# Attention block on one core: order of the joins, norm work beside reciprocals, and the place of one copy

## The chip, the core and the metric

The kernel runs on one core of a Trainium2 chip. A core has five engines that work side by side, each through its own queue in order: TensorE (PE in the profile; its weight loads are listed apart as PEld), VectorE (DVE), ScalarE (ACT), GpSimd (POOL) and SyncE (SP), which here only issues DMAs. They wait for each other by semaphores. The metric is the device time of one execution in microseconds; lower is better. A profile of one execution gives every instruction's start and duration, and times below that look like 601.73 are microseconds from the start of that execution's span.

## The reference

Four images of 512 channels and 48 x 48 = 2304 positions go through group normalisation, multi-head self-attention over the positions, a projection and a residual addition:

```python
hn = _group_norm(x, gn_scale, gn_bias)                    # 32 groups
qkv = einsum('oc,bchw->bohw', qkv_w, hn) + qkv_b          # float32
q, k, v = qkv.reshape(b, 3, 8, 64, t).astype(float16)     # 8 heads of 64
w = softmax(einsum('bhct,bhcs->bhts', q * s, k * s))      # s = 64 ** -0.25
a = einsum('bhts,bhcs->bhct', w, v).astype(float32)
out = einsum('oc,bchw->bohw', proj_w, a) + proj_b
return x + out
```

(shortened: `split` of q, k and v along the second axis, bias broadcasts left out.)

## The kernel before

Everything below is the fast path; a general path stands behind a flag and is not taken with these inputs.

**Tiling.** Channels lie on the 128 partitions in NC = 4 chunks. Heads are taken in pairs (two times 64 rows fill the partitions), 4 pairs an image, 16 pairs g in all. Query positions are cut into five blocks j, four of 512 and a last one of 256. A unit of the stream is one pair, one block and BURST = 3 tiles of keys: a block of 512 has six units, the last block three, 27 units a pair and 432 in all. The loop `for n in range(end)` issues one unit of scores each time and works on older units behind it.

**A unit.** `scores` multiplies k and q into PSUM banks ps (L955; three banks in turn) and ScalarE takes the exponential of each into the tile p (L962), three exps of 1024 columns. `values`, two units behind, multiplies v and p into the bank av (L980). The sum of the exponentials, by which the result is divided, is built on VectorE: `add`, one unit behind, adds p into the running sum acc (L1009, 3 x 1024 columns at once). When the block's last unit has been added, the three parts of acc are joined by two more additions of 1024 columns, L1012; those are the joins. Two units later `add_up` sums acc over the partitions with a matmul against ones into the bank sl (L1032), and `rows` copies sl to slx (L1048) and sends the sums by DMA to the tile sums. In the meantime av has been copied to avx (L989). av and sl use one and the same bank in turn, so sl waits for the copy avx, and the next block's av for the copy slx.

**After the block.** Counted from the block's last unit, `invert` comes four units later: it takes the reciprocal of the sums (L1077) and sends it to DRAM; POOL checks the sums' range beside it (L1070, L1071). A unit later `spread` fetches the reciprocals, broadcast over partitions, into the tile ib, and a unit after that `divide` multiplies avx by ib on POOL and writes the pair's result att (L1096). POOL's divisions thus stand six units behind the block's end.

**Work beside the units.** A list `beside` holds the other chains of matmuls in a fixed order: q and k of later pairs (L709, evacuated with bias and scale by VectorE at L719), v (L760, evacuated at L768), and the output projection of the image before (L844, evacuated with bias and residual at L871). Each chain uses the single bank pw, so a chain cannot begin before the one before it has been evacuated. `fill(n)` is called in every unit: it first lets VectorE do some norm tasks of the next image, then issues pieces of chains, paced by a credit so that the list is used up evenly. The norm tasks are statistics (L608, estimated 0.65 us each), their aggregation (L612), the scale of the groups (L622 to L634 with the square root of L631 on POOL), the coefficients (L641 to L653) and the normalisation in place (L660, estimated 0.55 us each). How many of them run is set by `room`, in estimated microseconds; tasks are taken while it is above zero. It is smaller in a unit whose predecessor ended a block (`ended(n - 1)`, where the joins are) and in the one that has the copy slx (`ended(n - BEHIND - 1)`), and larger when the next chain has to wait for the norm itself (`idle`).

**Order in a unit.** VectorE gets, in this order: the addition or, at a block's end, the addition and both joins; then (after `values`) avx; the reciprocal; the norm tasks; the evacuation of the chain that this unit finishes. All of it is issued into VectorE's queue in this order, and the queue is not reordered.

**The projection's input.** Before the chains of a projection, `att32` widens four blocks of att, one for each pair, from 16 to 32 bits (tiles a). Pairs 0 and 1 are copied by ScalarE (L838), pairs 2 and 3 by POOL (L836); `beside_exps` names the pairs of POOL. In the last image some blocks are projected in two parts: the first three pairs (FIRST) early, the last one at the end. A chain reads the pairs in order, two matmuls each (weights split in a high and a low part, whi and wlo).

Of the kernel before, what the change touches and what calls it, by code (L numbers as in the profile page):

```python
# [27 lines left out]
NC = C // P  # L28
# [4 lines left out]
BURST = 3  # L33
BEHIND = 2
# [433 lines left out]
def fast_path(  # L468
# [311 lines left out]
    now = [0]  # L780
# [37 lines left out]
    def left_over(b, j):  # L818

        return b == B - 1 and j >= NQ - 2  # L820

    beside_exps = range(NC // 2, NC)

    def att32(b, j, pairs=range(NC)):
        o, n = QBLOCKS[j]
        for c in pairs:
            if left_over(b, j):
                t = xpool.tile([P, n], F32R, tag=f"x{c}_{j}", name=f"a32_{b}_{j}_{c}")
            else:
                t = work.tile(  # L830
                    [P, QB], F32R, tag=f"a32_{c}", bufs=1, name=f"a32_{b}_{j}_{c}"
                )
            at32[b, j, c] = t[:, :n]
            source = atts[b * NPAIR + c][:, o : o + n]
            if c in beside_exps and not (pairs == LAST and left_over(b, j)):
                nc.gpsimd.tensor_copy(at32[b, j, c], source)  # L836
            else:
                nc.scalar.copy(at32[b, j, c], source)  # L838
# [13 lines left out]
    FIRST, LAST = range(NC - 1), range(NC - 1, NC)  # L852
# [80 lines left out]
    av, acc, pts, avx, sums, rowd, ibs = {}, {}, {}, {}, {}, {}, {}  # L933
# [31 lines left out]
    def values(u):  # L965
# [21 lines left out]
        if last and u is not stream[-1]:  # L987
            avx[g, j] = work.tile([P, QB], F32, tag="avx", name=f"avx_{g}_{j}")
            nc.vector.tensor_copy(avx[g, j][:, :n], av[0][:, :n])  # L989

    def add(u):

        g, j, k, last = u
        pt = pts[u]
        if k == 0:
            acc[g, j] = [pt]
            return
        if j >= NQ - 2 and g == NG - 1 and (last or j == NQ - 1):
            acc[g, j].append(pt)
            return  # L1000
        before = acc[g, j][0]
        if k == 1:
            acc[g, j] = [
                work.tile(
                    [P, BURST, 2, QB], F16, tag="acc", bufs=1, name=f"acc_{g}_{j}"
                )
            ]
        t = acc[g, j][0]
        nc.vector.tensor_tensor(t, before, pt, ALU.add)  # L1009
        if last:  # L1010
            for r in range(1, BURST):
                nc.vector.tensor_tensor(t[:, 0], t[:, 0], t[:, r], ALU.add)  # L1012
            acc[g, j] = [t[:, :1]]

    def add_up(g, j, bank=None, more=False):

# [27 lines left out]
    def rows(g, j, sl):  # L1044

        o, n = QBLOCKS[j]
        sx = work.tile([P, QB], F32, tag="rows", name=f"slx_{g}_{j}")
        nc.vector.tensor_copy(sx[:, :n], sl[:, :n])  # L1048
        sm = small.tile([P, 2, QB // P], F32, tag="sums", name=f"sums_{g}_{j}")
        for h in range(2):  # L1050
            nc.sync.dma_start(sm[:, h, : n // P], sx[h * D : h * D + 1, :n])
        sums[g, j] = sm
        return sx
# [38 lines left out]
        ibs[g, j] = ib  # L1092

    def divide(g, j):
        o, n = QBLOCKS[j]
        nc.gpsimd.tensor_tensor(  # L1096
            atts[g][:, o : o + n],
            avx.pop((g, j))[:, :n],
            ibs.pop((g, j))[:, :n],
            ALU.mult,  # L1100
        )
# [37 lines left out]
    def do_tasks(room):  # L1139
        while tasks and tasks[0][0] <= now[0] and room > 0:  # L1140
            _, us, run = tasks.popleft()
            run()
            room -= us
# [42 lines left out]
    for b in range(B):  # L1186
        g = b * NPAIR
# [113 lines left out]
    def issue():  # L1301
        us, run = beside.pop(0)[:2]
        run()
        credit[0] -= us

    def fill(n):

        idle = beside and beside[0][4] and not beside[0][4]()
        if ended(n - 1):
            room = 1.1 if idle else 0.0
        elif ended(n - BEHIND - 1):
            room = 1.1 if idle else 0.5
        else:
            room = 2.4 if idle else 1.1
        do_tasks(room)
        rate, work = 0.0, 0.0
        for us, _, _, _, _, _, need in beside:  # L1320
            work += us
            left = min(need * per_pair, len(stream) - 4) - n
            rate = max(rate, work / max(left, 1))
        credit[0] = min(credit[0] + rate, 4.0)
        closed = False
        while beside:
            us, _, first, last, when, after, _ = beside[0]
            if after > n or (first and closed) or (when and not when()):
                break
            if us > 0.1 and credit[0] < (0.0 if first and last else us / 2):  # L1330
                break
            issue()
            closed = closed or last

    def wanted(g):

        while any(p[6] <= g for p in beside):
            while loads:
                loads.popleft()[1]()
            while tasks:  # L1340
                tasks.popleft()[2]()
            issue()
            credit[0] = max(credit[0], 0.0)

    ended = lambda n: 0 <= n < len(stream) and stream[n][3]
# [5 lines left out]
    def block_at(n):  # L1351

        return stream[n][:2] if ended(n) and n not in soon else None

    def load_due(n):
        while loads and loads[0][0] <= n:
            loads.popleft()[1]()

    for n in range(end):
        now[0] = n  # L1360
        summed = block_at(n - BEHIND - 1)
        if not summed:
            load_due(n)
        wanted(stream[n][0])
        scores(stream[n])
        if summed:

            rows(*summed, add_up(*summed))
            load_due(n)
        if n > 0:  # L1370
            add(stream[n - 1])
        if summed:

            fill(n)
        if n >= BEHIND:
            values(stream[n - BEHIND])
        if block_at(n - BEHIND - 2):
            check_sums(*block_at(n - BEHIND - 2))
            invert(*block_at(n - BEHIND - 2))
        if block_at(n - BEHIND - 3):  # L1380
            spread(*block_at(n - BEHIND - 3))
        if block_at(n - BEHIND - 4):

            divide(*block_at(n - BEHIND - 4))
        if not summed:
            fill(n)
        if n - BEHIND in soon:
            g, j = stream[n - BEHIND][:2]
            sx = rows(g, j, add_up(g, j))
            if n - BEHIND == soon[1]:  # L1390
                divide_here(g, j, sx, avx[g, j], nc.gpsimd)
        if n - BEHIND - 1 == soon[0]:
            check_sums(g, j)
            invert(g, j)
        if n - BEHIND - 2 == soon[0]:
            spread(g, j)
            divide(g, j)
    g, b, j = NG - 1, B - 1, NQ - 1
    n = QBLOCKS[j][1]
    values(stream[-2])  # L1400
    while loads:
        loads.popleft()[1]()
    check_sums(g, NQ - 2)
    att32(b, NQ - 2, LAST)

    def last_banks(name):
# [5 lines left out]
    sl = held[:, 0, :]  # L1412
    add_up(g, j, sl, more=True)
    add(stream[-1])
    values(stream[-1])
    add_up(g, j, sl)
# [125 lines left out]
```

## Time and profile before

| what | us |
|---|---|
| median of 3 runs | 1608.62 |
| lowest and highest run | 1607.31, 1609.03 |
| the profiled execution | 1608.58 |
| its span, first to last instruction | 1606.8 |
| one exp of 1024 columns (L962), mean | 1.025 |
| one addition of 3072 columns (L1009), mean | 1.794 |
| one join (L1012), mean of 156 | 0.746 |
| one evacuation r (L871), mean of both shapes | 0.693 |
| one POOL division (L1096), mean of both shapes | 1.607 |
| one copy of 512 columns on POOL (L836), mean of 31 | 0.801 |
| the same on ScalarE (L838), mean of 33 | 0.635 |
| one unit of the stream, median distance of two starts of ps | 3.25 |

How to read it: the page lists busy time by engine, the chain of work that ended last (followed back from the last instruction, at each step to what released it), and groups of instructions by line and tile names. Lines in order of time give the start, the duration of what is merged in the line, engine, line, operation, out<-in, shapes and count, and in brackets how long the engine had been idle and who ended that. The page lists idle time of an engine only where something it waited for is seen; matmuls are pipelined, and their ends are modelled. The difference of 1.8 us between the profiled execution and its span lies around the span.

### The profile page before, as it was taken

The numbers are of one execution on the slowest core, as the hardware profiler recorded it, in microseconds if no ns is written. First come the engines' busy times: TensorE is split into PE (matmuls) and PEld (weight loads), VectorE is DVE, ScalarE is ACT, GpSimd is POOL, SyncE is SP. The second block draws the span as 40 slices with busy tenths as digits, with TensorE's granted clock in tenths as the row PEclk, the third lists the DMA queues.
The fourth block names the chain that finished last, engine by engine and source line by source line (L and its number), as shares of the span: only waits on it lengthen the run. The fifth ranks groups of instructions, "written<-read, shape, count | busy, mean of one in ns | idle before, by whom it ended". The sixth has DMA issues, their size and how long they took to land.

```text
span 1606.8 us, 28320 instructions
## 1 busy us (share of the span) xinstructions
PE 1579.1 (98%) x11500; PEld 691.7 (43%) x11500; DVE 1140.3 (71%) x1301; ACT 1267.1 (79%) x1360; POOL 329.5 (21%) x459
## 2 busy tenths in 40 slices
PE   6999999999999999999999999999999999999997
PEld 2533434443333534555333354455533334435554
DVE  6267668866676678887666666898766666667775
ACT  3077777888888888888888888887878888888895
POOL 1011202211121222322111121231212121222232
PEclk9999999999999999999999999999999999999999
DMA  7002021000000024421000001452100000016424
GB/s 220 3 14 65 13 60 28 18 14 11 14 15 14 12 69 119 142 67 28 11 14 18 14 12 41 114 156 84 28 15 15 15 15 11 15 31 188 125 67 128
DMA packets 94896, 82.10 MB, mean 51 GB/s; under 512 B 50852, under 2 KB 60964, under 8 KB 94756
## 3 DMA queue, kind: packets, MB, share of 16 engines
q1 hardware_dynamic: 92724, 78.35, 17.8%
q8 instruction: 92, 1.51, 0.4%
q10 hardware_dynamic: 1904, 1.84, 0.4%
q14 instruction: 48, 0.39, 0.1%
q0 software_dynamic: 128, 0.01, 0.0%
HBM read 60.70 MB, written 19.17 MB: 50 GB/s over the span
## 4 chain that ended last, share of the span: by engine, by line
PE 92%; DVE 3%; DMA 2%; ACT 1%; issue 1%; POOL 1%; SPq 0%; ACTq 0%; DVEq 0%; POOLq 0%
PE pqk L709 29%; PE ps L955 19%; PE av L980 19%; PE pv L760 15%; PE pr L844 7%; PE sl L1032 2%; PE ps L709 1%; ACT p L962 1%; DVE acc L1009 1%; DMA r<-x_dram 1%; DMA wqkv<-qkv_wT_dram 0%; DVE acc L1012 0%; DVE r L871 0%; DMA ib<-row 0%; POOL a L836 0%
## 5 line engine op out<-in xcount | busy, mean ns | idle before, releaser
L962 ACT ACTIVATE p<-ps 128x1024 f16<-128x1024 f32 x1296 | 1233.4, 1025 | 309.2 <-PE ps L955 307.0
L1009 DVE TENSOR_TENSOR acc<-acc,p 128x3072 f16<-128x3072 f16 x270 | 484.3, 1794 | 54.4 <-ACT p L962 51.9
L709 PE MATMUL pqk<-x,wqkv 128*64 128x512 f32 (+1 forms) x2464 | 517.2, 550 | 0.2
L980 PE MATMUL av<-p,v 128*64 128x512 f16 (+1 forms) x2880 | 360.8, 364 | 0.4 <-DVE slx L1048 0.3
L955 PE MATMUL ps<-q,k 64*128 64x512 f16 (+1 forms) x2880 | 356.0, 358 | 1.2 <-ACT p L962 0.8
L760 PE MATMUL pv<-wqkv,x 128*64 128x256 f32 x2304 | 267.5, 379 | 0.0
L709 PEld LDWEIGHTS pqk<-x,wqkv 128*64 128x64 f32 x2464 | 170.1, 137 | 211.1 <-issue 161.0
L1070 POOL TENSOR_SCALAR in<-sums 128x8 f32<-128x8 f32 (+1 forms) x158 | 103.2, 653 | 724.7 <-DMA sums<-slx 718.0
L955 PEld LDWEIGHTS <-k 64*128 64x128 f16 x2880 | 105.9, 94 | 287.9 <-issue 238.9
L980 PEld LDWEIGHTS <-v 128*64 128x64 f16 x2880 | 131.3, 109 | 213.4 <-issue 168.8
L1096 POOL TENSOR_TENSOR att<-avx,ib 128x512 f16<-128x512 f32 (+1 forms) x78 | 125.3, 1607 | 436.9 <-DMA ib<-row 393.9
L760 PEld LDWEIGHTS pv<-wqkv,x 128*64 128x64 f32 x2304 | 161.6, 137 | 85.6 <-DVE v L768 0.6
L1009 DVE TENSOR_TENSOR acc<-p,p 128x3072 f16<-128x3072 f16 x79 | 138.1, 1748 | 0.0
L844 PE MATMUL pr<-a,whi 128*128 128x512 f32 (+1 forms) x311 | 122.0, 400 | 4.0 <-POOL a L836 2.2
L1012 DVE TENSOR_TENSOR acc<-acc 128x1024 f16<-128x1024 f16 x156 | 116.3, 746 | 5.3
L844 PE MATMUL pr<-a,wlo 128*128 128x512 f32 (+1 forms) x311 | 113.6, 373 | 0.0
L719 DVE TENSOR_SCALAR q<-pqk,bqkv 128x512 f16<-128x512 f32 (+1 forms) x79 | 54.7, 693 | 72.6 <-PE pqk L709 72.4
L719 DVE TENSOR_SCALAR k<-pqk,bqkv 128x512 f16<-128x512 f32 (+1 forms) x75 | 52.0, 693 | 73.3 <-PE pqk L709 73.1
L768 DVE TENSOR_TENSOR v<-pv,bv 128x512 f16<-128x512 f32 x72 | 49.5, 688 | 75.4 <-PE pv L760 75.2
L1048 DVE COPY slx<-sl 128x512 f32<-128x512 f32 (+1 forms) x79 | 50.6, 641 | 67.5 <-PE sl L1032 67.5
L989 DVE COPY avx<-av 128x512 f32<-128x512 f32 (+1 forms) x79 | 50.6, 640 | 56.9 <-PE av L980 56.7
L871 DVE SCALAR_TENSOR_TENSOR r<-pr,bproj,r 128x512 f32<-128x512 f32 (+1 forms) x80 | 54.8, 693 | 38.6 <-PE pr L844 36.0
(79 smaller groups left out, 477.0 us busy)
## 6 DMA issues: line engine op xcount, KB each, us to landing
r<-x_dram SPq DMA_DIRECT2D x72, 256.0 KB, 3.7
out_dram<-r SPq DMA_DIRECT2D x69, 256.0 KB, 2.5
ib<-row SPq DMA_DIRECT2D x126, 128.0 KB, 3.1
x<-x_dram SPq DMA_DIRECT2D x62, 256.0 KB, 4.1
x<-x_dram SPq DMA_DIRECT2D x16, 128.0 KB, 4.9
sums<-slx SPq DMA_DIRECT2D x128, 2.0 KB, 2.1
ib<-row SPq DMA_DIRECT2D x30, 64.0 KB, 3.1
wqkv<-qkv_wT_dram SPq DMA_DIRECT2D x2, 768.0 KB, 6.9
```

The lines of the kernel that those rows point to most:

```text
L709: nc.tensor.matmul(pw[0][lo : lo + D, :n], wqkv[:, c, w0 + lo : w0 + lo + D], hn[b, c, j], start=(c == 0), stop=(c == NC - 1),)
L719: nc.vector.tensor_scalar(qk[g][part][:, o : o + n], pw[0][:, :n], bqkv[:, col : col + 1], SCALE, ALU.add, ALU.mult,)
L760: nc.tensor.matmul(pw[0][lo : lo + D, a, :], hn[b, c, i * P // QB][:, at + lo : at + lo + D], wqkv[:, c, 2 * C + half * C // 2 :][:, : C / ...
L844: nc.tensor.matmul(ps[:, :n], w[:, c, bass.ts(m, P)], at32[b, j, c], start=(i == 0), stop=(i == len(steps) - 1),)
L871: nc.vector.scalar_tensor_tensor(xt[:, i], places[i], bias, xt[:, i], ALU.add, ALU.add)
L955: nc.tensor.matmul(ps[:, h, a * n : (a + 1) * n], kt[rows, bass.ts(i, P)], qt[rows, o : o + n], start=True, stop=True,)
L962: nc.scalar.activation(pt[:, r], ps, AF.Exp)
L980: nc.tensor.matmul(av[0][lo : lo + D, :n], vv[b, pr // 2][:, i, pr % 2 * P + lo : pr % 2 * P + lo + D], pt[:, r, h, a * n : (a + 1) * n], ...
L1009: nc.vector.tensor_tensor(t, before, pt, ALU.add)
L1012: nc.vector.tensor_tensor(t[:, 0], t[:, 0], t[:, r], ALU.add)
L1070: nc.gpsimd.tensor_scalar(t, sm, limit, None, op)
L1096: nc.gpsimd.tensor_tensor(atts[g][:, o : o + n], avx.pop((g, j))[:, :n], ibs.pop((g, j))[:, :n], ALU.mult,)
```

## The change

Three edits. `add` issues the first join at once and puts the second into a queue `joins`, which the loop empties behind `fill(n)`, thus behind the evacuation of the chain that this unit finishes. In `fill`, the unit four behind a block's end, the one with the reciprocal, gets the smaller `room` (0.5, or 1.1 when idle, where it had 1.1 and 2.4). `att32` lets ScalarE copy pairs 0, 1 and 2 when a division has been issued in the same unit, and POOL pair 3 alone; in other units the split stays at two and two.

```diff
-    beside_exps = range(NC // 2, NC)
+    divided = [-1]
+
+    def beside_exps():
+
+        return range(NC - 1 if divided[0] == now[0] else NC // 2, NC)
...
-            if c in beside_exps and not (pairs == LAST and left_over(b, j)):
+            if c in beside_exps() and not (pairs == LAST and left_over(b, j)):
...
+    joins = deque()
+
     def add(u):
...
         if last:
-            for r in range(1, BURST):
+            acc[g, j] = [t[:, :1]]
+
+            def join(r):
                 nc.vector.tensor_tensor(t[:, 0], t[:, 0], t[:, r], ALU.add)
-            acc[g, j] = [t[:, :1]]
+
+            for r in range(1, BURST - 1):
+                join(r)
+            joins.append(lambda: join(BURST - 1))
...
     def divide(g, j):
+        divided[0] = now[0]
...
-        elif ended(n - BEHIND - 1):
+        elif ended(n - BEHIND - 1) or ended(n - BEHIND - 2):
             room = 1.1 if idle else 0.5
...
         if not summed:
             fill(n)
+        while joins:
+            joins.popleft()()
```

The order of instructions in the built programs shows what comes of it. TensorE's and SyncE's instructions stand in the same order in both. On VectorE the same 5631 instructions stand in another order: of 78 pairs of joins, 59 now have other work between them. Of the norm work, some statistics and normalisations of images 1 to 3 move to a later unit, and so do the aggregation in images 1 and 3 and the group scale in image 2. Two copies of pair 2 go from POOL to ScalarE: one in image 1, block 2, and one in image 3, block 3.

## The prediction

> **What bounds the kernel now.** I read the page's busy line and chain first, then TensorE's waits, then the order of time at each place where TensorE starts late.
>
> ```profile
> PE 1579.1 (98%) x11500; PEld 691.7 (43%) x11500; DVE 1140.3 (71%) x1301; ACT 1267.1 (79%) x1360; POOL 329.5 (21%) x459
> PE 92%; DVE 3%; DMA 2%; ACT 1%; issue 1%; POOL 1%; SPq 0%; ACTq 0%; DVEq 0%; POOLq 0%
> PE pr L844 <- POOL a L836: 2.2, 3, 1.6
> PE pr L844 <- DVE r L871: 1.0, 2, 0.5
> PE pr L844 <- DVE q L719: 0.6, 1, 0.6
> ```
>
> TensorE is busy for 98% of the span and carries 92% of the chain, at a granted clock of 0.998. So no saving on another engine counts unless TensorE was waiting for it. Its waits in the steady part are few and have names: the copies a (L836) on POOL and the evacuations r and q on DVE. Because matmul ends are modelled, the waits view understates them; I measured them from starts. In an undisturbed unit the first matmul of a chain starts 0.77 us after the first av matmul (0.67 us for a pqk chain after av), and a full projection chain takes 2.06 us from its start to the next ps matmul. What exceeds this is lost. Four places show the kinds of loss.
>
> ```profile
> 1484.08 2.72 POOL L1096 TENSOR_TENSOR att<-avx,ib 128x512 f16<-128x512 f32 x1 [3.69 <-DVE r L871]
> 1485.68 2.39 DVE L1012 TENSOR_TENSOR acc<-acc 128x1024 f16<-128x1024 f16 x2
> 1487.99 0.74 DVE L871 SCALAR_TENSOR_TENSOR r<-pr,bproj,r 128x512 f32<-128x512 f32 x1
> 1488.78 0.50 PE L844 MATMUL pr<-a,whi 128*128 128x512 f32 x1 [0.48 <-DVE r L871]
> ...
> 1039.55 1.26 DVE L608 BATCH_NORM_STATS2 st<-x 128x6 f32<-128x512 f32 x2
> 1040.72 0.47 DVE L719 TENSOR_SCALAR q<-pqk,bqkv 128x256 f16<-128x256 f32 x1
> 1041.24 0.51 PE L844 MATMUL pr<-a,whi 128*128 128x512 f32 x1 [0.55 <-DVE q L719]
> ...
> 1069.50 1.75 DVE L1009 TENSOR_TENSOR acc<-acc,p 128x3072 f16<-128x3072 f16 x1
> 1069.59 3.14 POOL L836 CAST a<-att 128x512 fp32r<-128x512 f16 x2
> 1071.77 0.50 PE L844 MATMUL pr<-a,whi 128*128 128x512 f32 x1 [0.33 <-POOL a L836]
> 1072.79 0.50 PE L844 MATMUL pr<-a,whi 128*128 128x512 f32 x1 [0.28 <-POOL a L836]
> ...
> 1516.23 1.15 ACT L838 CAST a<-att 128x512 fp32r<-128x512 f16 x2
> 1517.26 2.87 ACT L962 ACTIVATE p<-ps 128x1024 f16<-128x1024 f32 x3
> 1517.56 2.34 POOL L1096 TENSOR_TENSOR att<-avx,ib 128x256 f16<-128x256 f32 x1 [7.57 <-DMA ib<-row]
> 1519.85 1.07 POOL L836 CAST a<-att 128x512 fp32r<-128x512 f16 x1
> 1520.97 0.50 PE L844 MATMUL pr<-a,whi 128*128 128x512 f32 x1 [1.58 <-POOL a L836]
> ```
>
> The first shows two joins (L1012), the first of them held up by a POOL division, ahead of an evacuation that TensorE waits for. The second shows two statistics (L608) behind a reciprocal, ahead of an evacuation. The third shows a pair of POOL copies drawn out to 3.14 us beside a DVE addition. The fourth shows a POOL copy behind a division that waited for its DMA.
>
> **What the Trainium skill says.** "SBUF — State Buffer", section "Who interferes with whom": a DVE instruction with two SBUF inputs and a GpSimd instruction that reads SBUF exclude each other, whoever starts first holds the pair for its whole instruction, and PE and ACT never wait there. The trace agrees: a POOL copy of 512 columns takes 0.61 us alone, but the first of the pair above ended 0.47 us after the addition did; a join takes 0.69 us alone and 1.64 to 1.67 us beside a division. The evacuations have one SBUF input at most and stayed at 0.69 to 0.75 us everywhere. "ScalarE: Activation LUTs", section "What ACT_TABLE_LOAD costs": 186 ns plus 0.833 ns a column, back-to-back instructions overlapping by about 93 ns. For 512 columns that is 0.61 us, of which 0.52 us is new time; here a copy takes 0.64 us and its successor starts 0.51 us after it. I use 0.51.
>
> **The change part by part.** TensorE's and SP's instructions keep their order, and TensorE's waits are the same but for two copies that now come from ACT. So nothing is added on the bound; only lateness can change. No DMA is added or moved past another on its queue.
>
> A, the joins. 78 blocks have a second join; in 59 of them other DVE work now stands between the joins, mostly the evacuation. DVE's work is the same, and the evacuation ends up to 0.69 us (join plus gap, 0.72) sooner. It pays where TensorE was late behind it; the excess over 0.77 or 0.67 us: q at 601.73, 0.29 plus 0.05 in its chain; r at 644.55, 0.54; at 677.75, 0.14; at 1097.08, 0.19; at 1466.42, 0.12; at 1488.78, 0.55; at 1542.70, 0.05. Example: at 1488.78 the first join ends at 1487.34, the evacuation can follow at 1487.38 and end at 1488.12, and 0.05 us of handover (as between 1488.73 and 1488.78) gives 1488.17, before TensorE's own 1488.23. Each of the others fits in the same way; the sum is 1.93 us. The first join stays ahead and may still meet the lock, so 1.5 to 1.95. The second join now delays avx, L989, behind it: no cost, because avx cannot begin before the last av matmul is done. At 601 us the old second join ended at 601.02; the new one runs from 600.94 to 601.63, avx still starts at 601.72. If that cover went, sl (first matmul at 604.36) still leaves 1.9 us. Two late evacuations stay, since nothing before them changes: v at 278.91 behind the coefficients (0.32) and r at 655.80, which starts with DVE idle (0.13).
>
> B, the norm work. In the unit of the reciprocal one statistic instead of two is issued; the rest moves one unit on. At 1041.24 the loss over 0.77 is 0.62. With one statistic (0.68) after 1039.55, q ends at about 1040.60, TensorE starts at 1040.65 against 1040.62: gain 0.60, at least 0.3 if the sums' DMA behind the reciprocal comes later. The pushed-on work costs nothing where DVE idles before the next evacuation (r at 1043.42 waited 0.56 us for TensorE). The tightest place is near 1069 us, where the aggregation (four instructions, 0.64 us) now shares a unit with the group scale: r there ends at about 1070.13 to 1070.22 instead of 1069.58, and TensorE needs it at 1070.19. I take nothing; 0.05 is the bound there, and up to 1.5 us for such places that I have not found.
>
> C, the third copy on ACT. It applies twice only, in the units of 1068 and 1516 us. At 1516: the chain starts at 1518.19 and a six-matmul chain takes 1.60 us (1523.16 to 1524.76), so ps would follow at 1519.79 instead of 1521.64: 1.85 us are lost. The copy on ACT runs from 1517.26 to about 1517.9, its att block is ready (division at 1505.23), and the third pair is wanted at 1519.23. But the three exps behind it move by 0.51 and end at 1520.64, and the third ps pair needs the bank of the last one: it is wanted at 1520.22 and starts at 1520.69, 1.39 us before its 1522.08 of now. Gain 1.39; 0.9 if the exps slip more, 1.85 if not at all. At 1068: chain 1070.24 to ps 1073.45 is 3.21, so 1.14 are lost. The third pair comes from ACT in time (1069.97). The fourth stays on POOL behind rstd (L631), which B makes 0.6 us later: the copy falls behind the addition, which then runs from about 1070.1 to 1071.85, and ends 0.47 after it at 1072.3. One wait instead of two: the fourth pair starts at 1072.36, not 1072.79. Gain 0.42, between nothing and 1.14 (if POOL gets the lock first).
>
> Sum: 1.93 + 0.60 + 1.39 + 0.42 = 4.34 us. The profiled execution took 1608.58 (span 1606.8 and 1.8 around it), so 1604.2; the median of the three is 1608.62, the same within 0.04. Forecast 1604.3.
>
> **Rivals.** (1) The waits come back elsewhere: the fourth copy waits as long as both did (0 at 1068), ACT's late exps leave 0.9 at 1516, A gives 1.5, B 0.6, and shifted norm work costs 0.6 in new places: 2.4 us, 1606.2. For it: ACT is 79% busy, and TensorE already waits for exps after two copies (1535.32, 0.42 us). Against it: seven sites of A need nothing but order. (2) Slower, by one mechanism: avx, and with it the bank for sl, comes late behind the second join in every separated block. 0.15 us in each of 59 is 8.9, less 4.3: 1613.2; it decides from 4.3/59 = 0.07 us a block. For it: the joins can be held to 1.67 us by a division. Against it: the 1.9 us of room above, and TensorE waits for avx in one place, 0.2 us. (3) All of it comes: C gives 1.85 and 1.14, 5.5 us in all, 1603.1. (4) The edit hardly acts: 19 of 78 blocks keep adjacent joins, two copies of 38 move; but the losing places are among those that do change.
>
> **How the numbers follow.** Forecast 0.53, rival 1 0.25, rival 2 0.07, rival 3 0.15; (4) is inside rival 1. This kernel's runs lie within 0.11%, and 0.2% is 3.2 us. Sum of low ends with new waits of 1.5: 1.5 + 0.3 + 0 + 0.9 - 1.5 = 1.2 us, 1607.4; sum of high ends: 1.95 + 0.62 + 1.14 + 1.85 = 5.6, 1603.0. With 0.5 us of run spread I give 1602.5 to 1607.5. Faster: the forecast, rival 3, and nothing of rival 1: 0.68; same 0.25; slower 0.07.
>
> **What would show it.** Right: at the seven places of A the chain starts 0.77 (0.67) us after av; the wait "PE pr <- POOL a" shrinks from 2.2 to about 0.5 us and one for ACT's exps appears near 1517 us; TensorE's busy sum stays near 1579. Wrong: new waits of PE for avx, slx or x, or exps late by more than 0.5 us.

## The result and the profile after

Over 11 runs of each kernel the median fell from 1608.62 us to 1604.55 (1603.33 to 1605.11): ratio 0.9974, 95% interval 0.9966 to 0.9983. The forecast was 1604.3. The profiled execution took 1605.03 us, with a span of 1603.3.

First the busy line and the chain, from the page of the changed kernel:

```profile
PE 1577.8 (98%) x11500; PEld 692.1 (43%) x11500; DVE 1138.1 (71%) x1301; ACT 1268.0 (79%) x1362; POOL 325.6 (20%) x457
PE 94%; DVE 3%; ACT 1%; DMA 1%; issue 0%; POOL 0%; SPq 0%; DVEq 0%
```

TensorE does the same work as before, and two copies have moved from POOL (459 instructions to 457) to ACT (1360 to 1362). What was gained are waits, as this view of TensorE's waits shows (what waited, for whom: us in all, times, longest):

```profile
PE ps L959 <- ACT p L966: 1.1, 3, 0.5
PE pr L848 <- DVE r L875: 0.6, 2, 0.4
PE pr L848 <- POOL a L840: 0.4, 1, 0.4
PE sl L1043 <- DVE avx L993: 0.2, 1, 0.2
```

The wait for POOL's copies fell from 2.2 to 0.4 us, the one for evacuations r from 1.0 to 0.6, and the one for q (0.6) is gone. One wait for exps is new. (Lines moved: the copies 836 and 838 are now 840 and 842, 844 is 848, 871 is 875, 955 is 959, 962 is 966, 989 is 993, 1009 is 1015, 1012 is 1020, 1077 is 1088, 1096 is 1108; in some variants below they stand a line or two off that.) The same four places as in the prediction, in order of time:

```profile
1481.90 2.42 DVE L1015 TENSOR_TENSOR acc<-acc,p 128x3072 f16<-128x3072 f16 x1
1484.36 0.69 DVE L1020 TENSOR_TENSOR acc<-acc 128x1024 f16<-128x1024 f16 x1
1484.96 0.74 DVE L875 SCALAR_TENSOR_TENSOR r<-pr,bproj,r 128x512 f32<-128x512 f32 x1
1485.62 0.68 DVE L1020 TENSOR_TENSOR acc<-acc 128x1024 f16<-128x1024 f16 x1
1486.23 0.50 PE L848 MATMUL pr<-a,whi 128*128 128x512 f32 x1
...
1037.32 0.17 DVE L1088 RECIPROCAL inv<-sums 128x4 f32<-128x4 f32 x1
1037.41 0.66 DVE L608 BATCH_NORM_STATS2 st<-x 128x6 f32<-128x512 f32 x1
1038.07 0.48 DVE L719 TENSOR_SCALAR q<-pqk,bqkv 128x256 f16<-128x256 f32 x1
1039.47 0.50 PE L848 MATMUL pr<-a,whi 128*128 128x512 f32 x1
...
1068.29 0.72 POOL L631 TENSOR_TENSOR rstd<-veps,mhalf 128x2 f32<-128x2 f32 x1 [0.74 <-DVE both L634]
1068.86 1.75 DVE L1015 TENSOR_TENSOR acc<-acc,p 128x3072 f16<-128x3072 f16 x1
1068.96 2.12 POOL L840 CAST a<-att 128x512 fp32r<-128x512 f16 x1
1071.14 0.51 PE L848 MATMUL pr<-a,whi 128*128 128x512 f32 x1 [0.42 <-POOL a L840]
...
1513.68 1.67 ACT L842 CAST a<-att 128x512 fp32r<-128x512 f16 x3
1514.75 0.73 POOL L1108 TENSOR_TENSOR att<-avx,ib 128x256 f16<-128x256 f32 x1 [7.31 <-DMA ib<-row]
1515.03 2.07 DVE L1015 TENSOR_TENSOR acc<-acc,p 128x3072 f16<-128x3072 f16 x1
1517.24 0.60 PE L959 MATMUL ps<-q,k 64*128 64x512 f16 x4
1518.15 0.39 PE L959 MATMUL ps<-q,k 64*128 64x512 f16 x2 [0.30 <-ACT p L966]
```

In the first, the evacuation stands between the joins, and TensorE shows no idle time before its chain. In the second, q is evacuated by 1038.55, 0.9 us before TensorE wants its bank. In the third, one POOL copy instead of two lies beside the addition, and TensorE waits once. In the fourth, ACT makes three copies (1.67 us), the chain runs through, and the ps matmuls behind it are split by a wait for late exps.

To see all of it, the start of each of the 432 units was compared between two traces; where the difference of the starts jumps, time was gained or lost. This table has the jumps in us, relative to the first trace of the kernel before (positive is gained). A place has the time at which the unit behind it starts in that first trace: 1043 is the prediction's loss at 1041.24, 1073 the one near 1069, and 1516 to 1525 its fourth place; 676 holds norm work, and 658, 1054 and 1558 are evacuations that wait for a residual's DMA. All kernels of the section below are in it; "seven" is the sum at the prediction's seven places of the joins.

| kernel | seven | 1043 | 1073 | 1516 to 1525 | 676 | 658 | 1054 | 1558 | rest and start | all |
|---|---|---|---|---|---|---|---|---|---|---|
| the prediction's forecast | 1.93 | 0.60 | 0.42 | 1.39 | 0 | 0 | 0 | 0 | 0 | 4.34 |
| changed, first trace | 1.91 | 0.63 | 0.35 | 1.36 | -0.20 | 0.11 | -0.48 | -0.29 | 0.27 | 3.66 |
| changed, second (a_again) | 1.92 | 0.63 | 0.35 | 1.37 | -0.11 | -0.63 | -0.01 | -0.01 | 0.19 | 3.70 |
| changed, third (a_third) | 1.92 | 0.63 | 0.37 | 1.36 | -0.10 | 0.11 | 0.00 | -0.01 | 0.19 | 4.47 |
| joins alone (e1) | 1.91 | 0.63 | 0.01 | 1.84 | 0.00 | 0.05 | 0.00 | -0.01 | 0.02 | 4.45 |
| norm alone (e2) | 0.13 | 0.63 | -0.66 | 1.36 | -0.16 | 0.13 | -0.02 | -0.01 | -0.58 | 0.82 |
| copy alone (e3) | 0.19 | -0.13 | 1.01 | 1.37 | -0.01 | -0.81 | -0.02 | -0.08 | -0.39 | 1.13 |
| joins and copy (e4) | 1.91 | 0.63 | 1.01 | 1.37 | 0.00 | 0.12 | 0.00 | -0.01 | -0.18 | 4.85 |
| joins and copy (e4_again) | 1.90 | 0.58 | 0.97 | 1.38 | -0.01 | -0.68 | -0.01 | -0.01 | 0.02 | 4.14 |
| before, second trace (b_again) | -0.11 | -0.03 | -0.69 | 0.00 | -0.01 | -0.31 | -0.85 | -0.01 | 0.10 | -1.90 |
| reciprocal first (e9) | 0.00 | 0.63 | -0.50 | 0.61 | 0.00 | 0.13 | -0.02 | -0.01 | 0.16 | 1.00 |
| copy once (e8) | 1.90 | 0.64 | 0.78 | 0.99 | -0.01 | 0.11 | 0.00 | -0.03 | -0.69 | 3.69 |
| both joins late (e5) | 1.90 | 0.62 | 0.37 | 1.37 | -0.01 | 0.12 | -0.01 | -0.05 | -0.45 | 3.86 |
| reload later (e7) | 1.91 | 0.63 | 0.35 | 1.37 | -0.01 | -0.65 | -0.51 | -0.01 | -0.33 | 2.75 |

The row of the changed kernel looks like the forecast, term by term. The rows below it show that two of these terms, at 1043 and at 1516, also come without the edit to which the prediction gave them. A row is one execution, and some lie off the median of their kernel: e2's is 0.9 us faster, those of e3, b_again and e7 are 1.9, 1.8 and 1.5 us slower. The column "all" is therefore not the gain of the kernel; that is the ratio of the medians.

### The profile page after: what moved, and what is told of

Read it like the earlier page. It is cut to its first block, busy times and chain, and to the rows that moved or that the text cites. A ratio compares the mean times of both kernels' runs of the same rounds, so it can differ in the third digit from the quotient of the medians.

```text
span 1603.3 us, 28319 instructions
## 1 busy us (share of the span) xinstructions
PE 1577.8 (98%) x11500; PEld 692.1 (43%) x11500; DVE 1138.1 (71%) x1301; ACT 1268.0 (79%) x1362; POOL 325.6 (20%) x457
## 3 DMA queue, kind: packets, MB, share of 16 engines
q10 hardware_dynamic: 1904, 1.84, 0.4%
## 4 chain that ended last, share of the span: by engine, by line
PE 94%; DVE 3%; ACT 1%; DMA 1%; issue 0%; POOL 0%; SPq 0%; DVEq 0%
PE pqk L709 29%; PE ps L959 19%; PE av L984 19%; PE pv L760 15%; PE pr L848 8%; PE sl L1043 2%; ACT p L966 1%; PE ps L709 1%; DVE acc L1015 1%; DVE st L608 1%; DMA row<-inv 0%; DMA r<-x_dram 0%; DMA x<-x_dram 0%; DVE r L875 0%; DVE grouped L627 0%
```

## The experiments

Theory T, from the prediction: each edit removes the losses at its own places, and the edits add up. Rival R, formed from the first comparison of traces: some of the losses hang on when a small DMA lands or who gets the lock, so that several edits can remove the same one, and an edit may be worth nothing beside another. Times of one group were taken on one chip, beside runs of the kernel before on it.

### The three edits by themselves, and two together

On this chip the kernel before had a median of 1606.9 us (1605.6 to 1610.82). Edits that are not named are put back as they were before; the diffs here are against the changed kernel.

**e1_joins**: the joins edit alone.

```diff
-            return range(NC - 1 if divided[0] == now[0] else NC // 2, NC)
+            return range(NC // 2, NC)
...
-        elif ended(n - BEHIND - 1) or ended(n - BEHIND - 2):
+        elif ended(n - BEHIND - 1):
```

> The kernel before with the join edit alone. Ledger theory (each change of the time is a TensorE lateness at a named place): the seven places of A lose their wait and nothing else changes, 1.9 us, so about 1606.7 against 1608.6; copy and norm places stay as before (1.14 us lost near 1070 us, 1.85 near 1521). Rival (the second join makes the copy avx late): some of it comes back, under 1.3 us gained, with TensorE waits for avx that before does not have.

Measured: 1604.54 us (1603.81 to 1606.32), ratio 0.9988 (0.9981 to 0.9994), span 1602.5. The seven places gave 1.91 us, as forecast. But 0.63 at 1043 and 1.84 at 1516 came too, without the edits that were to bring them. At 1516 POOL kept the copy, and it was in time:

```profile
1513.92 0.73 POOL L1108 TENSOR_TENSOR att<-avx,ib 128x256 f16<-128x256 f32 x1 [6.50 <-DMA ib<-row]
1514.59 0.61 POOL L840 CAST a<-att 128x512 fp32r<-128x512 f16 x1
1515.02 1.80 DVE L1015 TENSOR_TENSOR acc<-acc,p 128x3072 f16<-128x3072 f16 x1
```

In these three lines in order of time, division and copy are over or under way when DVE's addition starts; before, the division started with it, and the copy stood behind it. T fails here. That the moved joins won the place at 1516 does not follow, though, as e2 shows.

**e2_norm**: the norm edit alone; both joins at once.

```diff
-            for r in range(1, BURST - 1):
+            for r in range(1, BURST):
                 join(r)
-            joins.append(lambda: join(BURST - 1))
...
-            return range(NC - 1 if divided[0] == now[0] else NC // 2, NC)
+            return range(NC // 2, NC)
```

> The kernel before with the smaller norm room in the reciprocal's unit alone. Ledger theory: 0.63 us gained near 1041 us, given back near 676 us (0.20, the coefficients one unit later) and near 1054 us (0.48, a residual load lands late), and near 1070 us both POOL copies start 0.6 us later behind the root and fall behind the addition: 0.6 more lost there. Net 0.6 us slower, between 0.2 faster and 1.0 slower: about 1609.2. Additive theory (the edit is worth what the prediction gave it): 0.6 us faster, 1608.0.

Measured: 1608.85 us (1607.7 to 1609.92), ratio 1.0012 (1.0006 to 1.0019): slower, by more than expected. At 1043 it gains its 0.63, but it loses 0.66 at 1073, 0.16 at 676, 0.43 at 680 (inside "seven") and 0.30, 0.21 and 0.27 at 173, 325 and 347 us (in the rest). At 173, 325 and 680 work pushed one unit on moves the joins, and the evacuation behind them, 0.2 to 0.4 us later; at 1073 the aggregation stands in front of the evacuation. At 347 a join met a POOL division (1.64 us instead of 0.69), which may be chance. Its gains of 0.55 at 1491 (inside "seven") and 1.36 at 1516 have nothing to do with norm work: image 3 is the last one. The broadcast ib of the division near 1484 happened to land 0.53 us ahead of its unit there, where it landed 0.79 to 0.97 after it in the two traces of the kernel before; the division did not meet the join. At 1516 the lines in order of time are:

```profile
1517.49 0.73 POOL L1107 TENSOR_TENSOR att<-avx,ib 128x256 f16<-128x256 f32 x1 [6.74 <-DMA ib<-row]
1518.16 0.61 POOL L840 CAST a<-att 128x512 fp32r<-128x512 f16 x1
1518.33 2.05 DVE L1015 TENSOR_TENSOR acc<-acc,p 128x3072 f16<-128x3072 f16 x1
```

The division started 0.84 us ahead of the addition, where it started 0.01 ahead of it and 0.05 behind it in the two traces of the kernel before, and POOL's copy was in time with both joins in their old place. In e3 below, also with the old joins, the division was 0.75 us ahead. So an early division at 1516 does not need the moved joins. What they do change there is the next evacuation: in e2 it stands behind both joins and 0.49 is lost at 1525, in e1 it does not and nothing is lost. One trace of a kernel is thus no measure of an edit at such a place.

**e3_copy**: the copy edit alone.

```diff
-            for r in range(1, BURST - 1):
+            for r in range(1, BURST):
                 join(r)
-            joins.append(lambda: join(BURST - 1))
...
-        elif ended(n - BEHIND - 1) or ended(n - BEHIND - 2):
+        elif ended(n - BEHIND - 1):
```

> The kernel before with the third copy on ScalarE alone. Ledger theory: near 1521 us 1.36 gained (1.85 less 0.49 for the late exps); near 1070 us the one copy left on POOL starts at 1069.6 as the first did before and is ready when TensorE wants it, so all 1.14 us are gained where the combination had 0.35: 2.2 to 2.5 us in all, about 1606.2. Additive theory: what the combination showed, 1.7 us, 1606.9.

Measured: 1605.79 us (1604.83 to 1608.09), ratio 0.9993 (0.9985 to 1.0002), so the timing alone does not tell it from none, and it is less than the 2.2 to 2.5 us expected. In the trace it has 1.01 at 1073 and 1.37 at 1516, 2.4 in all, and loses 0.81 at 658 to a DMA (below). With the joins in their old place it also gained 0.29 at 603, one of the seven.

**e4_joins_copy**: joins and copy, without the norm edit.

```diff
-        elif ended(n - BEHIND - 1) or ended(n - BEHIND - 2):
+        elif ended(n - BEHIND - 1):
```

> The changed kernel without its norm edit. Ledger theory: 1.9 from the joins and 2.2 to 2.5 from the copies, 4.1 to 4.4 us: about 1604.3, and a span 0.4 to 0.9 us shorter than that of the changed kernel. Additive theory: 0.6 us slower than the changed kernel, 1605.2.

Measured: 1603.87 us (1603.46 to 1605.9), ratio 0.9982 (0.9975 to 0.9988), span 1601.9, the shortest of all traces. The trace has 4.85 us, and 1043 is won without the norm edit. At 1073 it gains 1.01 of the 1.14 us that were lost there, as these lines in order of time show:

```profile
1066.96 0.72 POOL L631 TENSOR_TENSOR rstd<-veps,mhalf 128x2 f32<-128x2 f32 x1
1067.54 1.74 DVE L1015 TENSOR_TENSOR acc<-acc,p 128x3072 f16<-128x3072 f16 x1
1067.63 2.12 POOL L840 CAST a<-att 128x512 fp32r<-128x512 f16 x1
1069.81 0.50 PE L848 MATMUL pr<-a,whi 128*128 128x512 f32 x1
```

The last POOL copy ends 0.47 us behind the addition here too, at 1069.75. TensorE just then wants it. In the changed kernel aggregation and group scale are in one unit, evacuation and addition come later, and the same copy is 0.42 us late.

### What repeats, and two variants

The kernel before had 1608.69 us (1606.69 to 1613.24) on this chip.

**b_again**: the kernel before, no edit.

> The kernel before, unchanged, timed against itself and traced a second time. It measures two things: what ratio the comparison gives for no change at all, and which of the late places of the first trace come again. Theory 1 (the late places belong to the order of the instructions): the losses of 0.6 us at 1041, 0.55 at 1489, 1.14 at 1069 and 1.85 at 1516 us are there again within 0.1 us each. Theory 2 (some of them depend on when a small DMA happens to land): the ones at 1041 and 1516 us are smaller by more than 0.5 us or gone, with the DMAs of the sums, the row or the broadcast landing 0.5 to 0.9 us sooner, and the others stay. Time: ratio 1.000 within 0.0007 in both.

Measured: 1608.79 us, ratio 1.0002 (0.9993 to 1.001). The seven places, 1043, and 1516 each lose the same again within 0.12 us. These are lines in order of time from this second trace:

```profile
1519.49 1.75 DVE L1009 TENSOR_TENSOR acc<-acc,p 128x3072 f16<-128x3072 f16 x1
1519.54 2.28 POOL L1096 TENSOR_TENSOR att<-avx,ib 128x256 f16<-128x256 f32 x1 [7.64 <-DMA ib<-row]
1521.77 1.07 POOL L836 CAST a<-att 128x512 fp32r<-128x512 f16 x1
1522.89 0.50 PE L844 MATMUL pr<-a,whi 128*128 128x512 f32 x1 [1.58 <-POOL a L836]
```

The division starts 0.05 us behind the addition, is held until the addition has ended (2.28 us instead of 0.73 in e1), and TensorE waits 1.58 us, exactly as in the first trace. So at these places theory 1 of the expectation holds. At 1073, which it counted among the fixed ones, it fails: 0.69 us more were lost. There the norm instruction L629, issued while a POOL division runs, ended 0.02 to 0.03 us after that division in both traces; the division came 0.83 us later in its unit in the second one, so L629 took 0.99 us instead of 0.28, and the evacuation and the copies behind it followed. e8 and e9 show the same (0.52 and 0.78 us). So a loss of 0.69 at 1073 can come with no norm edit. Of the others, 658 and 1054 lost 1.16 us more than in the first trace, to residuals that landed late.

**a_again**: the changed kernel, no edit.

> The changed kernel once more, on the chip of these runs, to stand beside the variants below. The ratio recorded first was 0.9974; expected 0.997 to 0.9985, about 1604.5 us where before is 1607 to 1608.6. In the trace: the losses at 1054 us (0.48, an evacuation that waited for its residual's DMA) and at 676 us (0.20) return if they belong to the order of the instructions; they are gone if the DMA landed late by chance. The norm edit by itself cost 1.9 us; if that cost stands in the full change too, this kernel is 0.5 to 0.7 us slower than the joins and the copy without the norm edit (1603.87 there).

Measured: 1604.41 us (1603.6 to 1605.35), ratio 0.9975 (0.9965 to 0.9984). The 0.48 at 1054 are gone, so they were chance; at 676 it is 0.11 of 0.20. At 658 the trace is 0.74 us behind the first one of the changed kernel (0.63 lost instead of 0.11 gained), and this was followed to its DMA. In order of time:

```profile
654.56 0.75 DVE L875 SCALAR_TENSOR_TENSOR r<-pr,bproj,r 128x512 f32<-128x512 f32 x1 [1.94 <-PE ps L959]
655.36 0.50 PE L848 MATMUL pr<-a,whi 128*128 128x512 f32 x1 [0.68 <-DVE r L875]
```

DVE sat idle before this evacuation though the matmuls named in brackets had long been done: it waited for its residual, which landed at 654.47, 1.39 us after its unit's start. That load is always issued 3.77 to 3.83 us before the unit. In the 14 traces it landed between 0.82 us before and 1.57 us after the unit's start, and the time at 658 follows it: every trace in which it landed over 1 us after the start (b_again, e3, e4_again, a_again, e7) loses 0.31 to 0.81 there, and no other trace does.

**e7_reload**: the changed kernel, image 3's last reload one unit later.

```diff
-        loads.append((now[0] + 1, run))
+        later = (b, j) == (B - 1, NQ - 1)
+        loads.append((now[0] + (2 if later else 1), run))
```

> The changed kernel, with the reload of image 3's last block of x one unit later, so that the broadcast of the reciprocals stands before those four loads in SP's queue, not behind them. Theory DMA: the reciprocals' row took 6.53 us behind the four loads of 128 KB, the broadcast and the residual's load behind it came late, and 0.48 us was lost at 1054; with the loads moved the row lands within 3 to 4 us of its issue, the residual lands before 1049.5, and the 0.48 are gained: 1604.0 if the changed kernel is 1604.5. Rival: the row's latency does not come from those loads; the row still takes over 5 us and the time stays within 0.2 us. Second rival: the x loads themselves become late for their statistics, a new wait of DVE, up to 1 us slower.

Measured: 1604.55 us (1603.43 to 1606.02), ratio 0.9972 (0.9963 to 0.9982). Inconclusive: the 0.5 us expected of it did not come, and the row's time does not tell the loads from chance. The row took 4.64 us, not 6.53, but in a_again it took 4.92 with the loads in their old place. The residual was then the one behind the four loads, landed late (1051.01), and 0.51 was lost at 1054 as in the first trace of the changed kernel.

**e5_both**: the changed kernel with both joins behind the evacuation.

```diff
-            for r in range(1, BURST - 1):
-                join(r)
-            joins.append(lambda: join(BURST - 1))
+            for r in range(1, BURST):
+                joins.append(lambda r=r: join(r))
```

> The changed kernel with both joins behind the evacuation, not only the second. Theory: where the first join held the evacuation beside a division (1.64 us at 1485.68) nothing is lost any more, but the changed kernel has no loss left at the joins' places above 0.1 us, so the same within 0.3 us. Rival 2 of the prediction (avx late behind the joins): with two joins, 1.4 us, ahead of avx the cover of 1.9 us to sl is nearly used, and where a division holds a join it is exceeded; sl or the next av waits 0.2 us or more in several blocks: 0.5 to 3 us slower. If it is slower, TensorE's waits for avx and slx grow from 0.5 us in sum.

Measured: 1604.92 us (1604.18 to 1606.53), ratio 0.998 (0.9971 to 0.9988). The same as the changed kernel within its spread. TensorE's waits for avx and slx are 0.2 and 0.3 us, as with one join behind, so the path of rival 2 through avx to the bank for sl does not act even with twice the work ahead of avx. But the late avx is not free. At 1081 this trace alone lost 0.37 us:

```profile
1075.69 0.74 DVE L875 SCALAR_TENSOR_TENSOR r<-pr,bproj,r 128x512 f32<-128x512 f32 x1
1076.49 0.51 PE L848 MATMUL pr<-a,whi 128*128 128x512 f32 x1 [0.30 <-DVE r L875]
```

With two joins ahead of it, avx started 0.40 us later in its unit than in the changed kernel; the norm work behind it and this evacuation moved by 0.39, and TensorE waited for them.

### The reciprocal, the second copy, and the norm edit once more

The kernel before had 1608.44 us (1606.47 to 1611.16) on this chip.

The traces showed one thing that the joins edit does beside the evacuation. A block of 256 has three units. The unit in which its joins stand is therefore the one that takes the reciprocal of the block of 512 before it. In the kernel before, that reciprocal stood behind both joins; in the changed one it passes the second. e9 does this and nothing else.

**e9_recip_first**: joins ahead of the evacuation, as before; where a reciprocal is in the unit, the second join behind it. The diff is against e1, from which the emptying of the queue behind the evacuation is taken out as well.

```diff
             joins.append(lambda: join(BURST - 1))
+            if not block_at(now[0] - BEHIND - 2):
+                joins.popleft()()
...
             invert(*block_at(n - BEHIND - 2))
+            while joins:
+                joins.popleft()()
```

> Neither the norm edit nor the copy edit, and both joins stay ahead of the evacuation. The only change: where a unit has joins and a reciprocal (a block of 256 ended, and the block of 512 before it gets its reciprocal), the second join stands behind the reciprocal. Theory: the joins edit also works through the reciprocals, because it lets them pass one join (0.73 us), and with them row, broadcast, sums and division come sooner, SP being in order. Then row 9_3 is issued 3.9 us after its unit starts (4.61 before), the sums of 9_4 leave 8.8 to 9.1 us after it (about 10.0 to 10.3 before), the loss of 0.6 us at 1041 is gone, and the division near 1517 can start ahead of the addition there (up to 1.85 us less 0.49 for an evacuation behind the joins); the seven places behind the joins keep their losses. In the trace 1.5 to 2.5 us less than before; in the ratio 0.9985 to 0.9995. Rival: the losses at 1041 and 1516 went away with the evacuations' earlier ends, not with the reciprocals: both are there as before, ratio 1.000.

Measured: 1607.64 us (1606.07 to 1609.67), ratio 0.9994 (0.9985 to 1.0002). First two groups of lines in order of time from the kernel before, then the same from e9:

```profile
1028.88 1.42 DVE L1012 TENSOR_TENSOR acc<-acc 128x1024 f16<-128x1024 f16 x2
1030.22 0.20 DVE L1077 RECIPROCAL inv<-sums 128x8 f32<-128x8 f32 x1
1030.44 0.38 SPq L1079 DMA_DIRECT2D row<-inv  x1
1032.16 2.43 SPq L1089 DMA_DIRECT2D ib<-row  x2
1035.80 1.14 SPq L1051 DMA_DIRECT2D sums<-slx  x2
```

```profile
1028.47 0.69 DVE L1020 TENSOR_TENSOR acc<-acc 128x1024 f16<-128x1024 f16 x1
1029.08 0.20 DVE L1090 RECIPROCAL inv<-sums 128x8 f32<-128x8 f32 x1
1029.20 0.69 DVE L1020 TENSOR_TENSOR acc<-acc 128x1024 f16<-128x1024 f16 x1
1029.30 0.38 SPq L1092 DMA_DIRECT2D row<-inv  x1
1031.00 1.11 SPq L1102 DMA_DIRECT2D ib<-row  x2
1034.22 1.14 SPq L1064 DMA_DIRECT2D sums<-slx  x2
1038.05 0.17 DVE L1090 RECIPROCAL inv<-sums 128x4 f32<-128x4 f32 x1
```

The unit starts at 1025.84 in the first and 1025.42 in the second, so the row leaves 4.60 and 3.88 us after it, one join sooner. The broadcast and the next sums stand behind it in SP's queue, in order, and the sums leave 9.96 and 8.80 us after it. The next reciprocal then starts 12.63 instead of 13.61 us after the start (before, DVE had been idle 1.15 us for these sums), and q's evacuation with two statistics in front is in time: 0.63 at 1043, with no norm edit and all the seven places untouched (0.00). The sums gain 1.16 us where the join explains 0.7; the rest was not followed. All 14 traces agree: in the ten whose reciprocal passes a join the sums leave 8.2 to 9.0 us after the start of the unit and 1043 is won, in the four others 9.8 to 10.3 us, and of these only e2, with the norm edit, wins it. At 1516 only 0.61 came, since the division started 0.08 us before the addition and POOL's copy fell behind it. The trace has 1.00 us where 1.5 to 2.5 were expected, and the interval of the ratio includes 1, so the gain rests on the traces and not on the timing.

**e8_copy_once**: joins and copy without the norm edit, the third copy on ACT in image 1 alone (against e4).

```diff
-        return range(NC - 1 if divided[0] == now[0] else NC // 2, NC)
+        return range(NC - 1 if divided[0] == now[0] < 300 else NC // 2, NC)
```

> Joins edit and the third copy on ScalarE in image 1 alone (near 1068 us); in the last image (near 1516 us) pair 2 stays on POOL; no norm edit. Theory: with the joins edit the division near 1514 is done before the addition takes the lock, so POOL's copy is in time, and the copy on ScalarE only makes three exps late by 0.5 us. So this is 0.45 to 0.5 us faster than joins and copy together, and the fastest of all, 4.5 to 5 us less than before in the trace. Rival: the division is late in some executions; then this kernel loses up to 1.85 us there and the copy on ScalarE is worth keeping.

Measured: 1604.58 us (1603.39 to 1607.22), ratio 0.9976 (0.9966 to 0.9985). The trace has 3.69 us where 4.5 to 5 were expected, and the rival was right. The lines in order of time:

```profile
1514.45 0.73 POOL L1108 TENSOR_TENSOR att<-avx,ib 128x256 f16<-128x256 f32 x1 [7.13 <-DMA ib<-row]
1514.91 1.89 DVE L1015 TENSOR_TENSOR acc<-acc,p 128x3072 f16<-128x3072 f16 x1
1515.13 2.14 POOL L840 CAST a<-att 128x512 fp32r<-128x512 f16 x1
1517.32 0.50 PE L848 MATMUL pr<-a,whi 128*128 128x512 f32 x1 [0.60 <-POOL a L840]
```

The division came 0.46 us ahead of the addition, the copy 0.22 us behind it, so the copy took 2.14 us. In e1 the division was 1.10 us ahead, and the copy took 0.61. With the copy on ACT the place gives 1.36 to 1.38 us in all eight traces of kernels that have it. Without it the gain follows the lead of the division over the addition: 0.00 in the two traces of the kernel before, where the addition got ahead (lead 0.01 and -0.05 us, division 2.3 us long), 0.61 with 0.08 us (e9), 0.99 with 0.46 (e8), 1.36 with 0.84 (e2, after the 0.49 that its joins cost at 1525) and 1.84 with 1.10 (e1).

**e4_again** and **a_third**: joins and copy, and the full change, side by side.

> Joins and copy edits without the norm edit, a second time, beside the full change on the same chip. Theory: the norm edit gives nothing once the joins have moved (the loss at 1041 is gone without it) and costs 0.66 us near 1069 (an aggregation and a group scale in one unit) and 0.2 near 676; so this is 0.6 to 1.2 us faster than the full change. Rival: the norm edit's 0.6 us at 1041 are real in the full change: this is 0.5 us slower or equal.

> The full change beside the three variants, on one chip: about 4 us less than before, 0.6 to 1.2 us slower than without its norm edit, 1.1 to 1.7 us slower than with the copy in image 1 alone.

Measured: 1603.91 us (1603.31 to 1604.35), ratio 0.997 (0.9958 to 0.9982), against 1604.41 us (1603.39 to 1605.58), ratio 0.9975 (0.9965 to 0.9984). The medians differ by 0.5 us in the expected direction, a little less than the 0.6 to 1.2 expected, and the intervals overlap, so the timing alone does not settle it. The full change was also expected 1.1 to 1.7 us behind e8; it was 0.2 us ahead. The traces do at one place: at 1073 the full change and its two variants gave 0.35 to 0.37 in five traces, the kernel without the norm edit 1.01 and 0.97, and e8 and e3, also without it, 0.78 and 1.01. The span of a_third is the shorter one (1602.1 against 1602.4), because e4_again met the late residual at 658 (-0.68 against 0.11). Joins and copy without the norm edit has the lowest median in both groups, here by about half a microsecond.

## Why the prediction was right, and where it was not

**A, the joins: right, to the size.** 1.93 us forecast, 1.90 to 1.92 in all nine traces of kernels that have this edit, and -0.11 to 0.19 in the four others. That avx has room behind one join held. With two (e5) the room to sl still held, but an evacuation behind avx came late, which neither the prediction nor its rival 2 had looked at.

**A, what was left out.** The prediction looked only at what stands between the joins and TensorE's next chain. It did not name the reciprocal, which the second join lets pass as well, nor the row, broadcast and sums behind it on SP. e9 shows that this alone is enough for the 0.63 at 1043.

**B, the norm work: this step failed.** "At 1041.24 the loss over 0.77 is 0.62. With one statistic ... gain 0.60" gives the right size, and the edit does it by itself (e2). But in the full change it is not B's gain: e1 and e4 have it without B. The cost of the pushed-on work, of which the prediction says "I take nothing" (with up to 1.5 us in its range for places not found), failed with it. By itself the edit made the kernel slower, ratio 1.0012 (1.0006 to 1.0019), some 1.9 us. In the full change the losses at 173, 325 and 680 vanish: the second join no longer stands in front of those evacuations. What stays is about 0.6 at 1073 in all five traces of kernels with all three edits, and 0.1 to 0.2 at 676 in the three of the full change itself but not in e5 and e7: the moved norm work met a POOL division there in some executions. The prediction had found the place near 1069 and named 0.05 as the bound for the evacuation; the larger cost was in its own part C, where it took the fourth copy's fall behind the addition as given and did not book the 0.6 us to B. e4, without B, has 1.01 there.

**C, the copies: sizes right.** 0.42 forecast at 1073, 0.35 to 0.37 measured; 1.39 forecast at 1516, 1.36 to 1.38 measured, with the exps late by 0.5 us as foreseen. The step of 0.51 us a copy on ACT, which the prediction took beside the 0.52 that it works out from the Trainium skill ("ScalarE: Activation LUTs", section "What ACT_TABLE_LOAD costs"), held here (three copies end to end 1.67 us, so 1.15 for two and 0.52 for the third). At 1516 the copy's gain is rather an insurance: POOL's copy is in time in some executions (e1, e2) and not in others (e8, e9), and on ACT it no longer matters. In the three traces of the changed kernel the division's lead over the addition was 0.28, -0.15 and 0.77 us; with the first two, judged by e8 and e9, POOL's copy would have been late.

What decides is who starts first. The Trainium skill, "SBUF — State Buffer", section "Who interferes with whom", states it as an exclusive lock: whoever issues first gets the shared ports for its whole instruction. The runs agree and add the price of the order: the copy takes 0.61 us when it starts 0.43 us before the addition (e1), 2.14 when it starts 0.22 us behind it (e8).

**The sum.** The median fell by 4.07 us. The terms gave 4.25 us in the first trace (1.91, 0.63, 0.35, 1.36), 4.34 forecast; late residuals at 1054 and 1558 and the norm work at 676 took 0.97 back, and small gains elsewhere gave 0.38. These late residuals are not in the prediction, which took "r at 655.80 ... starts with DVE idle" as a fixed 0.13. That the sum came out so close is in part luck. The 0.60 booked to B would have come with A alone, and B's cost of 0.6 at 1073 lay hidden in C's 0.42. Both were in the sum already, so the sum came out right, while the one edit that costs time stood in it as a gain. The prediction's own arithmetic has one slip: its sum of low ends is 1607.4, to which 0.5 for the spread of runs was to be added, and the range ends at 1607.5.

**Still open.** e1's trace has 4.45 us, but its ratio, 0.9988, is some 1.9 us. The kernel before ran at 1606.9 us on that chip, 1.5 to 1.8 less than on the others, and no trace of it was taken there; e2 and e3, with the joins in their old place, had an early division at 1516 on that chip, and e2 won 0.55 at 1491 too, so the kernel before may often win these places there; without its trace this is not shown. The gain of single edits is known to about 1 us for that reason, and how much of e1's 1.84 at 1516 is due to the joins is open. What makes the residual at 658 late in five traces of 14 was not found.

## What to carry to other kernels

When an instruction is moved, list everything that it lets pass or holds up on its engine, and follow each to its DMA: here a reciprocal that passed one join won as much as an edit made for the same stall. Before adding a second remedy for a stall, look whether the first one has removed it; the second then shows only its costs. Where two engines race for a lock or a DMA lands close to its need, take two traces or more, of both kernels, and treat the place as won only if a variant wins it every time.

## What was not expected of the hardware

A load of 256 KB (the residual that is wanted at 655 us), issued at the same point of the program within 0.06 us in all 14 traces, took from 2.96 to 5.34 us to land, and from 3.63 to 5.17 in the three traces of the changed kernel. The Trainium skill, "DMA: Bandwidth & Descriptors", section "Latency and other measured facts", names an HBM latency of 0.2 us on average and 2 us at high load; the spread of 1.5 us within one program is about of this size, but no run here shows its cause. The row of the reciprocals near 1038 us, 2 KB, took 4.19 to 6.53 us from issue to landing. In a kernel whose TensorE is busy for 98% of the span, the late residuals at 658 and 1054 account for 1.16 of the 2 us by which the spans of two executions of the kernel before differ (1606.8 and 1608.8), and a division that came 0.83 us later in its unit, at 1073, for another 0.69.
